# A graph layer on one core: edge groups in pairs, 24 of 32 rows stored, and the last chunk's node sums by a product on chip

## The chip, the cores and the metric

The kernel runs on one core of one Trainium2 chip. Its time is the device time of one execution in microseconds (us), the median of several runs. All arithmetic is in 32-bit floating point. TensorE is called PE here, VectorE DVE, ScalarE ACT, GpSimd POOL and SyncE SP.

## The reference

One layer over 10000 nodes of 512 features, with 160000 edges. The edges are sorted by `dst`; the graph sum of a node collects the transformed rows of its edges.

```python
xn = layernorm(x)                                   # 10000 x 512
h = xn @ gnn_W
agg = segment_sum(h[src] * edge_weight[:, None], dst)   # 160000 edges
gnn = relu(agg + gnn_bias)
mix = gamma_layernorm(linear_attention(xn, w_qkv, 8 heads) @ w_out.T, gamma)
x = x + gnn + mix
f = layernorm(x)
# one mixture of 6 experts for the whole input: router on the mean row, top 2
x = x + sum_e weight[e] * (gelu(f @ W1[e] + b1[e]) @ W2[e] + b2[e])
```

The kernel sums the rows of `xn` first and multiplies the sums by `gnn_W` afterwards. In the queries, the softmax is over the features of a head, in the keys over all nodes.

## The kernel before

**Nodes.** The 10000 rows are cut into 20 chunks: 19 of 512 rows (128 partitions by 4 rows, `SUB`), and a last one of 272 (68 by 4).

**Edges.** The edges lie in 1250 tiles of 128 edges. A *window* is a stretch of 32 (`WIN`) consecutive nodes; the first 384 windows (`PAIRED`) take two tiles each, the 482 later ones one tile each, 866 windows in all (`NW`). Four windows (`GROUP`) make a *group*, so there are 217 groups (`NQ`): 96 of eight tiles and 121 of four. `edges_in` issues, for each tile, one indirect DMA on POOL's queue (line 584) that gathers 128 rows of `xn` from memory (`msg`, 256 KB), and builds on DVE the 0/1 selection times the edge weight (`sel`, lines 590 and 592). `edges_summed` multiplies them on PE (line 602): four products with 32 output rows each, side by side in four column strips of the array. ACT copies the 128x512 result (`part`, line 605) and stores it to `part_d` (line 606), 256 KB a group. Where a node's edges go over the border of two windows, `carry` adds the first four rows of one window to the next, in memory, by an accumulating DMA on POOL's queue (line 674); `CARRIES` says at which windows such a carry is issued.

**Three stages.** In the first (to about 1110 us) keys and queries of all chunks are computed, the queries are turned and stored, and the context is summed. In the second, the row loop (about 1110 to 1905 us), each chunk gets its attention output (`attention`, product `po`), its node sums (`gathered`: an indirect DMA on POOL's queue, line 1018, that fetches rows of `part_d` by the list `row_of`; then a transpose, `at` to `aT`, and the product `pg` with `gnn_W`), bias, relu, the sum with `x`, and the row statistics for the next layer norm. `attention` runs three chunks ahead (`MIXED`). In the third stage, the feed-forward (from 1919 us), each chunk's rows come back from memory (`rows_in`), are normalised on ACT and turned on DVE (line 367), and go through the experts' products (line 243) in a form that needs fewer products and sums of weights made once (`sums_of_weights`, `w1_sum`).

**The order of the work.** PE's order is the order in which the program emits the instructions. The other engines are ordered by a planner that uses estimated costs; `behind(a, b)` ties one instruction behind another on its engine. The products of the edges are spread over the other products: after each product, `put_out` calls `work(us)`, which adds the product's estimated time and calls `edges_to` up to the group that is due at `ROW_PACE` = 0.96 us a tile. Before group i is multiplied, gathers are issued until more than `LATE` = 4 messages are held ready. `far_enough(c)` brings in the edges that chunk c's gather needs: `AT_HAND` lists up to which window the first n chunks need them. The last two chunks need all of them, so at chunk 17 (`NCH - 3`) `all_edges_in` multiplies all remaining groups in one go, issues the last carry, frees the edges' memory and loads the experts' weights; the gathers of chunks 18 and 19, and then the attention of chunk 19, follow.

In the trace, the visits to the edges in the row loop are of one group, except for a burst of four groups before the gather of chunk 17 and one of six at the end.

Of the kernel before, what the change touches and what calls it, by code (L numbers as in the profile page):

```python
# [17 lines left out]
P = 128  # L18
SQ = 32
# [6 lines left out]
GROUP = 4  # L26
WIN = P // GROUP
FAR = 1.0e5
EARLY = 2
# [6 lines left out]
ROW_PACE = 0.96  # L36
LATE = 4
MIXED = 3

AT_HAND = [(5, 320), (7, 384), (8, 424), (9, 472), (10, 520), (11, 560), (12, 604), (13, 640), (14, 680), (15, 716), (16, 752),  # L40
           (17, 788), (18, 820)]
CHAINED = 128
# [9 lines left out]
    (2, 2, 2), (2, 2, 1, 1), (2, 1, 1, 1, 1), (1, 1, 1, 1, 1, 1),  # L52
]


@with_exitstack
def gps_layer_kernel(
# [90 lines left out]
    NQ = -(-NW // GROUP)  # L148
    ZERO_ROW = NQ * P
    far_rows = -(-(N + P) // (8 * P)) * 8 * P  # L150
# [73 lines left out]
    def sums_of(o, a11, a12, a21, a22):  # L224

        nc.vector.tensor_tensor(o[0], a21, a22, ALU.add)  # L226
        nc.vector.tensor_tensor(o[2], a11, a21, ALU.subtract)  # L227
        nc.vector.tensor_tensor(o[1], o[0], a11, ALU.subtract)  # L228
        nc.vector.tensor_tensor(o[3], a12, o[1], ALU.subtract)

# [148 lines left out]
    def sums_of_weights():  # L379
        w1_sb, w1_sum = held_w["w1"], held_w["w1_sum"]  # L380
        p_half, q_half = slice(0, PAIRS * P), slice(PAIRS * P, 2 * PAIRS * P)
        sums_of([w1_sum[:, i] for i in range(4)], w1_sb[:, :KH, p_half], w1_sb[:, KH:, p_half],
                w1_sb[:, :KH, q_half], w1_sb[:, KH:, q_half])
# [4 lines left out]
    with ExitStack() as ph:  # L388
# [50 lines left out]
        jump = b_io.tile([P, NW], F32, name="jump")  # L439
        count = ep.tile([P, 3 + len(AT_HAND) + 2 * NCH], F32, name="count")  # L440
        small_norms = ep.tile([P, 2, KB], F32, name="small_norms")
        usable = ep.tile([P, 1], F32, name="usable")
        n_odd = ep.tile([1, 1], I32, name="n_odd")

        def edges_listed():
# [8 lines left out]
        def place_edges(dst_sb, row_sb):  # L454
# [16 lines left out]
            def by_window_of(t, per_window, o, op):  # L471
# [30 lines left out]
            yield  # L502
            nc.vector.scalar_tensor_tensor(good, place, float(WIN), good, op0=ALU.is_lt, op1=ALU.mult,
                                           accum_out=count[:, 0:1])
            yield
            nc.vector.tensor_scalar(good[:, :NW], gap, 0.0, None, op0=ALU.is_ge)
            yield
            nc.vector.scalar_tensor_tensor(good[:, : NW - 1], gap[:, : NW - 1], float(WIN // SUB), good[:, : NW - 1],
                                           op0=ALU.is_lt, op1=ALU.mult, accum_out=count[:, 1:2])
            yield  # L510
# [12 lines left out]

        def window_at(node, more):
            tile_no = NET * (node / N) ** 0.5 + more
            return min(max(int(tile_no / 2 if tile_no < 2 * PAIRED else tile_no - PAIRED), 0), NW)

        def span(c):
            return window_at(chunks[c][0], -SPARE), window_at(chunks[c][0] + SUB * chunks[c][1], SPARE)

        def spans_hold():
            for c, (b, r) in enumerate(chunks):
                for i, w, op, edge in ((0, span(c)[0], ALU.is_le, b), (1, span(c)[1], ALU.is_ge, b + SUB * r)):
                    at = 3 + len(AT_HAND) + 2 * c + i
                    nc.vector.tensor_scalar(count[:, at : at + 1], bases[:, w : w + 1], float(edge // SUB), None, op0=op)
# [60 lines left out]
        def edges_summed(i, batch, m, sel):  # L596

            pm = psum_e.tile([P, D], F32, name="pm")
            for j in range(batch):
                for h in range(GROUP):  # L600
                    k = h * batch + j
                    nc.tensor.matmul(pm[h * WIN : (h + 1) * WIN, :], sel[:, k, :], m[k] if k < len(m) else m[0],  # L602
                                     start=j == 0, stop=j == batch - 1, skip_group_check=True)
            part = pools["w"].tile([P, D], F32, name="part")
            nc.scalar.copy(part, pm)  # L605
            nc.scalar.dma_start(part_d[i * P : (i + 1) * P, :], part)

# [28 lines left out]
        def oddities():  # L636
# [8 lines left out]
            nc.vector.tensor_tensor(n_odd, n[:, 0:1], n[:, 1:2], ALU.add)  # L645

        def next_nodes():
            pn = psum.tile([P, 1], F32, name="pnext", tag="ps")
            nc.tensor.transpose(pn[:CHAINED], bases[0:1, 1 : CHAINED + 1], ident[0:1, 0:1])
            nc.vector.tensor_copy(nexts[:CHAINED], pn[:CHAINED])  # L650
# [25 lines left out]

        carried = []
        for i in range(PARTS):
            carried.append((past(CHAINED // GROUP, i * LAG), partial(carry_loads, i)))
            carried.append((past(CHAINED // GROUP, (i + 1) * LAG), partial(carry_chained, i)))  # L680
# [4 lines left out]
        pace = [PACE]  # L685
        ahead = [AHEAD]
        EARLY_TOTAL = PRODUCT * KB * ROWS_IN * 3 * KB

# [10 lines left out]
        def work(us):  # L699

            done[1] += us
            if not pools:

                normal_rows(int(done[1] / EARLY_TOTAL * (NCH + 1)) + 4 - len(normal))
                return
            edges_to(groups_of(int(done[1] / pace[0])))

# [13 lines left out]
        def all_edges(fp):  # L721
# [10 lines left out]
            for b in range(0, far_rows // P, 8):  # L732
                nc.sync.dma_start(view[:, b : b + 8, :], zero[:, None, :].to_broadcast([P, 8, D]))
            nc.vector.tensor_copy(row_of, four)
            dst_sb = fp.tile([P, NET], I32, name="dst_far")
            nc.sync.dma_start(dst_sb, dst)
# [120 lines left out]
        for c, (_, r) in enumerate(chunks):  # L857
# [51 lines left out]
            for cb in range(KB):  # L909
# [11 lines left out]
                if cb == KB // 2 - 1:  # L921
                    qT = b_io.tile([P, KB, SUB * P], F32, name="qT")
                    transposed(qT, qt, r, psum, "ps", by_act=range(KB) if c < EARLY else (1, 3))
                    nc.scalar.dma_start(qT_d[c], qT[:, :, : SUB * r])
            if c == CHECKED:
                next_nodes()
                oddities()
            if c >= CHECKED:
                find_rows(c, added)
                if c < 2 * CHECKED:  # L930
                    find_rows(c - CHECKED, added)
# [53 lines left out]
        pace[0] = ROW_PACE  # L985
        ahead[0] = LATE
        done[1] = tiles_of(done[0])[0] * ROW_PACE

# [8 lines left out]
        def far_enough(c):  # L997

            for n, w in AT_HAND:
                if c < n:  # L1000
                    edges_to(min(NQ, past(w // GROUP, lag_of(w) + LEAD) + 1))
                    return w * WIN
            assert not pools
            return ZERO_ROW + P

        def all_edges_in():
            edges_to(NQ)
            carry(CARRIES[-1], NW - 1)
            assert not carried
            pools.clear()  # L1010
            edge_ctx.close()
            experts_weights()

        def gathered(c):
            r = chunks[c][1]
            n_rows = far_enough(c)
            at = io.tile([P, SUB, D], F32, name="at", tag="at" if c < NCH - 1 else "qT")
            nc.gpsimd.indirect_dma_start(
# [20 lines left out]
        def attention(c, beside):  # L1039


            r = chunks[c][1]
            qT, xt = held.pop("last") if c == NCH - 1 else (queries_in(c), rows_again(c))
            ot = io.tile([P, SUB, D], F32, name="ot", bufs=MIXED + 2)
# [19 lines left out]
        for c, (_, r) in enumerate(chunks):  # L1064
            ot, at = mixed.pop(0), ats.pop(0)
            aT = io.tile([P, KB, SUB * P], F32, name="aT", bufs=1)

            if c == NCH - 3:
                all_edges_in()
                ats += [gathered(c + 1), gathered(c + 2)]  # L1070

            def nodes_rows():
                transposed(aT, at, r, psum, "ps", by_act=range(KB))

            if c + MIXED < NCH - 1:
                mixed.append(attention(c + MIXED, nodes_rows))
            elif c == NCH - 3:
                mixed.append(attention(NCH - 1, nodes_rows))
            else:
                nodes_rows()  # L1080
            if c < NCH - 3:
                ats.append(gathered(c + 1))
            if c == NCH - 4:
                held["last"] = queries_in(NCH - 1), rows_again(NCH - 1)

            for s in range(SUB):
                po = psum.tile([P, D], F32, name="pg", tag="ps")
                times(po, aT, s, r, wg)
                put_out(KB * PRODUCT)
                nc.vector.tensor_tensor(po[:r, :], po[:r, :], bias_b[:r], ALU.add)  # L1090
                nc.vector.scalar_tensor_tensor(ot[:r, s, :], po[:r, :], 0.0, ot[:r, s, :], op0=ALU.max, op1=ALU.add)
# [16 lines left out]
            if c == NCH - 3:  # L1108
                sums_of_weights()
            if c == NCH - 2:  # L1110
                io_f["in"] = ctx.enter_context(tc.tile_pool(name="f_in", bufs=1, reuse_waits="tile"))

                io_f["squares"] = io_f["in"].tile([P, P // SQ, P], F32, name="squares")
                for b in range(P // SQ):
                    nc.vector.tensor_copy(
                        io_f["squares"][:, b].rearrange("k (g t) -> k g t", t=SQ),
                        ident[:, None, b * SQ : (b + 1) * SQ].to_broadcast([P, P // SQ, SQ]))
                xn = rows_in(0)
                st = small.tile([P, P // SQ, 1, SUB, 2], F32, name="st_sq", bufs=1)
                stats_of_squares(st, 0)  # L1120
                for step in normalising(0, xn, st[:, :, 0]):
                    step()
                turn = turned_in(0, rows_turned(0, xn))
        in_order.close()
# [349 lines left out]
```

## Time and profile before

| | us |
|---|---|
| median of 3 runs | 3501.84 (3490.08 to 3503.91) |
| the profiled execution's own time | 3295.9 |
| its span, first to last instruction | 3294.2 |
| PE busy / POOL busy / DVE busy / ACT busy | 3187.5 / 1317.8 / 1772.1 / 834.1 |
| row loop's last edge product ends | 1845.0 |
| last product of the row loop ends | 1905.5 |
| first product of the feed-forward starts | 1919.0 |

The mean granted clock of TensorE in the profile is 0.985 of full speed. A view of groups gives for each kind of instruction its number, its busy time and mean duration in nanoseconds, and the idle time of its engine just before it with what ended that time. In a timeline, a line is a run of like instructions: its start, its length, and in brackets the idle time ahead of it. A matmul in 32-bit floating point shows as two records, and products with 32 output rows run four at a time.

### The profile page before, as it was taken

To read this page: it belongs to the slowest core of one execution; us is meant where nothing else is said; L and a number is where in the kernel's file an instruction comes from. 1 tells how busy PE (TensorE), PEld (TensorE's weight loads), DVE (VectorE), ACT (ScalarE), POOL (GpSimd) and SP (SyncE) were. 2 spreads that over 40 slices of the span, in tenths; PEclk is the share of its full clock that TensorE was granted. 3 is DMA by queue.
4 is the path that set the end of the run, shared out by engine and by line. 5 is a ranking of instruction groups with operands and counts; after the bars stand their busy time and mean duration, and the time that the engine had idled before them with its cause. 6 is when DMAs were issued, how large, how long until landed. Compare 5 with 4: busy or idle time off the path is not lost. (4 is left out here: it accounts for less than half of the span.)

```text
span 3294.2 us, 35223 instructions
## 1 busy us (share of the span) xinstructions
PE 3187.5 (97%) x12819; PEld 1898.0 (58%) x12819; DVE 1772.1 (54%) x3902; ACT 834.1 (25%) x1674; POOL 1317.8 (40%) x1421
## 2 busy tenths in 40 slices
PE   5899999999999999999999979999999999999998
PEld 3344444444443333333333358888888888888886
DVE  6655555555555366666665665455544554445532
ACT  5422222222222122222222132222222222222211
POOL 3377777777776777777777200000000000000000
PEclk8899999999999999999999989999999999999999
DMA  9678889888888999999999822121212212121111
GB/s 391 245 238 282 265 274 311 265 281 255 283 267 240 344 353 355 337 350 351 354 338 313 230 67 62 52 90 52 64 52 76 66 52 64 52 90 51 54 38 41
DMA packets 216728, 654.33 MB, mean 199 GB/s; under 512 B 34425, under 2 KB 74361, under 8 KB 188831
## 3 DMA queue, kind: packets, MB, share of 16 engines
q0 software_dynamic: 104096, 354.29, 32.9%
q1 hardware_dynamic: 69992, 175.33, 16.2%
q10 hardware_dynamic: 42452, 122.31, 9.6%
q8 instruction: 105, 1.72, 0.2%
q14 instruction: 83, 0.68, 0.1%
HBM read 491.21 MB, written 166.63 MB: 200 GB/s over the span
## 5 line engine op out<-in xcount | busy, mean ns | idle before, releaser
L584 POOL DMA_INDIRECT msg<-xn_d,src_sb x1250 | 1237.6, 990 | 422.9 <-issue 318.4
L602 PE MATMUL pm<-msg,sel 128*32 128x512 f32 x2504 | 357.7, 604 | 15.4 <-DMA msg<-xn_d,src_sb 14.4
L209 PE MATMUL pg<-wq,aT 128*128 128x512 f32 (+1 forms) x640 | 292.2, 604 | 0.0
L209 PE MATMUL po<-G,qT 128*128 128x512 f32 (+1 forms) x640 | 290.3, 600 | 1.4 <-DMA qT<-qT_d 1.4
L912 PE MATMUL pc<-xn,ek 128*128 128x512 f32 (+1 forms) x640 | 285.5, 596 | 0.0
L605 ACT COPY part<-pm 128x512 f32<-128x512 f32 x217 | 127.0, 585 | 618.3 <-PE pm L602 577.4
L602 PEld LDWEIGHTS pm<-msg,sel 128*32 128x32 f32 x2504 | 67.0, 109 | 273.0 <-issue 190.5
L209 PEld LDWEIGHTS pg<-wq,aT 128*128 128x128 f32 (+1 forms) x640 | 115.5, 188 | 176.1 <-issue 161.2
L243 PE MATMUL px<-xnT,w_sb 128*128 128x256 f32 (+1 forms) x800 | 204.9, 379 | 7.0 <-DVE u L1291 6.6
L209 PEld LDWEIGHTS po<-G,qT 128*128 128x128 f32 (+1 forms) x640 | 114.8, 187 | 164.7 <-issue 157.8
L166 DVE BATCH_NORM_STATS2 st<-ot 128x6 f32<-128x512 f32 (+1 forms) x160 | 110.4, 690 | 180.1 <-ACT ot L1053 179.3
L243 PE MATMUL p<-kq_sum,xs_b 128*128 128x512 f32 (+1 forms) x432 | 200.7, 600 | 0.0
L912 PEld LDWEIGHTS pc<-xn,ek 128*128 128x128 f32 (+1 forms) x640 | 118.0, 191 | 139.3 <-issue 131.4
L243 PE MATMUL px<-w_sb,hh 128*128 128x256 f32 (+1 forms) x800 | 185.8, 379 | 0.0
L243 PE MATMUL py<-xs,w_sum 128*128 128x256 f32 (+1 forms) x800 | 185.7, 375 | 0.0
L243 PE MATMUL py<-w_sum,hh 128*128 128x256 f32 (+1 forms) x800 | 179.2, 379 | 0.0
L243 PEld LDWEIGHTS px<-xnT,w_sb 128*128 128x128 f32 x800 | 150.8, 192 | 30.1 <-DVE u L1291 10.2
L243 PEld LDWEIGHTS px<-w_sb,hh 128*128 128x128 f32 (+1 forms) x800 | 150.2, 188 | 22.8
L243 PEld LDWEIGHTS py<-w_sum,hh 128*128 128x128 f32 (+1 forms) x800 | 150.0, 188 | 22.7
L243 PEld LDWEIGHTS py<-xs,w_sum 128*128 128x128 f32 x800 | 150.2, 191 | 20.1
L243 PEld LDWEIGHTS p<-kq_sum,xs_b 128*128 128x128 f32 (+1 forms) x432 | 78.0, 187 | 116.1 <-issue 89.6
L351 ACT ACTIVATE xn<-xn,st_all 128x128 f32<-128x128 f32 x288 | 114.8, 481 | 97.3 <-DMA xn<-x_d 97.3
(298 smaller groups left out, 4566.8 us busy)
## 6 DMA issues: line engine op xcount, KB each, us to landing
part_d<-part ACTq DMA_DIRECT2D x217, 256.0 KB
msg<-xn_d,src_sb POOLq DMA_INDIRECT x1250
xn<-in_x SPq DMA_DIRECT2D x19, 1024.0 KB
xn_d<-xn ACTq DMA_DIRECT2D x19, 1024.0 KB
qT_d<-qT ACTq DMA_DIRECT2D x19, 1024.0 KB
qT<-qT_d SPq DMA_DIRECT2D x19, 1024.0 KB
xt<-in_x SPq DMA_DIRECT2D x19, 1024.0 KB
x_d<-ot SPq DMA_DIRECT2D x19, 1024.0 KB
```

The costliest lines, as they stand in the source:

```text
L166: nc.vector.bn_stats(st[:r, s, :], t[:r, s, :])
L209: nc.tensor.matmul(po[:r, :], t[:, kb, s * r : (s + 1) * r], w[:, kb, :], start=kb == 0, stop=kb == KB - 1)
L243: nc.tensor.matmul(o, lhs[j], rhs[j], start=start and j == 0, stop=stop and j == n - 1, skip_group_check=True)
L351: nc.scalar.activation(xn[:, s, b * P : (b + 1) * P], xn[:, s, b * P : (b + 1) * P], AF.Identity, bias=st[:, b, s, 0:1], scale=st[:, b, s, ...
L584: nc.gpsimd.indirect_dma_start(out=m[k], out_offset=None, in_=xn_d, in_offset=bass.IndirectOffsetOnAxis(ap=src_sb[:, t0 + k : t0 + k + 1], ...
L602: nc.tensor.matmul(pm[h * WIN : (h + 1) * WIN, :], sel[:, k, :], m[k] if k < len(m) else m[0], start=j == 0, stop=j == batch - 1, skip_gro ...
L605: nc.scalar.copy(part, pm)
L912: nc.tensor.matmul(pc, ek[:r, s, cb * P : (cb + 1) * P], xn[:r, s, :], start=s == 0, stop=s == SUB - 1)
```

## The change

- **Groups in pairs.** In the row loop `work` advances the edges in steps of `VISIT` = 2 groups, and `LATE` is 8 for 4.
- **24 rows of 32.** From window 384 on (one tile per window), only 24 rows (`USED`) of a window are stored, by four DMAs per group on ACT's queue, where there was one. The check at the start that a tile's nodes fit its window is made with 24 for these windows. The eight rows that are not stored are set to zero once, after chunk 5 (`rest_cleared`: a memset on POOL and 16 DMAs on ACT's queue).
- **The last chunk on chip.** Groups from 211 on (`ON_CHIP`) keep their sums in the buffers `parts`; groups 214 to 216 are not stored at all. `nodes_on_chip` works out, once, which node each of their rows belongs to, `numbered` makes of it a 0/1 matrix per group, and `last_sums` multiplies the kept sums with it: this gives chunk 19's turned node sums directly. Two calls: for the first four groups (`FIRST_SUMS`), at the end of chunk 17; for the other two in chunk 19, where rows gathered from memory are added too (in the ordinary case all of them zero).
- **The end of the edges.** `AT_HAND` gets the entry (19, 853), so chunk 18 does not wait for all edges. At chunk 17 the edges run on with its products up to group 214, then come the first sums, and `all_edges_in` with the last two groups. The attention of chunk 19 moves ahead to chunk 16.
- **The way into the feed-forward.** The rows of chunk 0 are loaded in `all_edges_in`, ahead of the weights. `sums_of_weights` moves from chunk 17's end to chunk 18's, and the bias additions of chunk 19 are tied behind it on DVE.

```diff
-LATE = 4
+LATE = 8
+VISIT = 2
+FIRST_SUMS = 4
-           (17, 788), (18, 820)]
+           (17, 788), (18, 820), (19, 853)]
+    ON_CHIP = window_at(N, NET, chunks[-1][0], -3) // GROUP
+    STORED = -(-CARRIES[-1] // GROUP)
...
             nc.scalar.copy(part, pm)
-            nc.scalar.dma_start(part_d[i * P : (i + 1) * P, :], part)
+            if batch > 1:
+                nc.scalar.dma_start(part_d[i * P : (i + 1) * P, :], part)
+            elif i < STORED:
+                for h in range(GROUP):
+                    nc.scalar.dma_start(by_window[i * GROUP + h, :USED, :], part[h * WIN : h * WIN + USED, :])
...
+        def rest_cleared():
+            zero = pools["w"].tile([P, PER, D], F32, name="none", tag="on", bufs=1)
+            nc.gpsimd.memset(zero, 0.0)
+            for w in range(PAIRED, STORED * GROUP, P):
+                end = min(w + P, STORED * GROUP)
+                for q in range(USED, WIN, PER):
+                    nc.scalar.dma_start(by_window[w:end, q : q + PER, :], zero[: end - w])
...
-            edges_to(groups_of(int(done[1] / pace[0])))
+            stop = min(groups_of(int(done[1] / pace[0])), limit[0])
+            edges_to(done[0] + (stop - done[0]) // visit[0] * visit[0])
...
             if c == CHECKED:
+                rest_cleared()
+                nodes_on_chip()
...
         def all_edges_in():
             edges_to(NQ)
-            carry(CARRIES[-1], NW - 1)
+            ats.append(gathered(NCH - 2))
+            ats.append(gathered(NCH - 1))
...
+            io_f["in"] = ctx.enter_context(tc.tile_pool(name="f_in", bufs=1, reuse_waits="tile"))
+            rows_first = rows_in(0)
             experts_weights()
...
+        def numbered():
+            b, r = chunks[-1]
+            mine = io.tile([P, NQ - ON_CHIP + 1, SUB, r], F32, name="mine", tag="xt", bufs=1)
+            number = mine[:, NQ - ON_CHIP]
+            nc.gpsimd.iota(number, pattern=[[1, SUB], [SUB, r]], base=b, channel_multiplier=0,
+                           allow_small_or_imprecise_dtypes=True)
+            for g in range(NQ - ON_CHIP):
+                nc.vector.tensor_scalar(mine[:, g], number, node_of[:, g : g + 1], None, op0=ALU.is_equal)
+            return mine
+
+        def last_sums(o, mine, groups, at):
+            n = SUB * chunks[-1][1]
+            for kb in range(KB):
+                kbs = slice(kb * P, (kb + 1) * P)
+                pt = psum.tile([P, SUB * P], F32, name="pt", tag="ps")[:, :n]
+                for g in groups:
+                    nc.tensor.matmul(pt, parts[g // 3][:, g % 3, kbs], mine[:, g].rearrange("p s n -> p (s n)"),
+                                     start=g == groups[0], stop=at is None and g == groups[-1], skip_group_check=True)
+                if at is None:
+                    nc.scalar.copy(o[:, kb, :n], pt)
+                    continue
+                r = chunks[-1][1]
+                for s in range(SUB):
+                    nc.tensor.matmul(pt[:, s * r : (s + 1) * r], at[:r, s, kbs], ident[:r, :r],
+                                     start=False, stop=s == SUB - 1, skip_group_check=True)
+                nc.vector.tensor_tensor(o[:, kb, :n], o[:, kb, :n], pt, ALU.add)
...
-            if c + MIXED < NCH - 1:
+            if c + MIXED < NCH:
                 mixed.append(attention(c + MIXED, nodes_rows))
-            elif c == NCH - 3:
-                mixed.append(attention(NCH - 1, nodes_rows))
+            elif c < NCH - 1:
+                nodes_rows()
             else:
-                nodes_rows()
+                last_sums(aT_last, mine, range(FIRST_SUMS, NQ - ON_CHIP), at)
...
+            if c == NCH - 3:
+                limit[0] = ON_CHIP + FIRST_SUMS
...
+                if c == NCH - 1:
+                    behind(added, weights_summed)
...
             if c == NCH - 3:
-                sums_of_weights()
+                mine = numbered()
+                aT_last = io.tile([P, KB, SUB * P], F32, name="aT_last", tag="ot", bufs=MIXED + 2)
+                edges_to(limit[0])
+                last_sums(aT_last, mine, range(FIRST_SUMS), None)
+                rows_first = all_edges_in()
             if c == NCH - 2:
...
-                turn = turned_in(0, rows_turned(0, xn))
+                turn = turned_in(0, rows_turned(0, rows_first))
+                weights_summed = sums_of_weights()
```

## The prediction

> **What bounds the kernel now.** I start with the busy tenths of 40 slices (82.4 us each).
>
> ```profile
> PE   5899999999999999999999979999999999999998
> POOL 3377777777776777777777200000000000000000
> DMA  9678889888888999999999822121212212121111
> ```
>
> PE is full nearly everywhere, but POOL stands at 7 from about 165 us to 1840 us, and 7 is all it can show: the timeline of POOL has a message gather of 0.95 us and then 0.30 us of issue before the next. So I asked for POOL's groups in 1095 to 1840 us, the row loop that the change touches.
>
> ```profile
> L584 POOL DMA_INDIRECT msg<-xn_d,src_sb x530 | 529.4, 999 | 174.6 <-issue 134.7 <-DMA msg<-xn_d,src_sb 19.6 <-PE po L209 5.9
> L1018 POOL DMA_INDIRECT at<-part_d,row_of x18 | 17.0, 945 | 12.1 <-DMA part_d<-part_d 4.7 <-issue 4.3 <-DMA msg<-xn_d,src_sb 1.9
> L674 POOL DMA_DIRECT2D part_d<-part_d x12 | 11.7, 974 | 0.0
> ```
>
> In each: instructions, busy us, mean ns of one, idle us just before and what ended it. And three stages, as start:end, length, then busy us of PE, PEld, DVE, ACT and POOL, PE's clock, DMA share and GB/s:
>
> ```profile
> 1400.00:1500.00 100.00, 100.00 (x359) 38.89 (x360) 61.56 (x161) 24.56 (x47) 74.95 (x76) 1.00 0.97 352
> 1820.00:1840.00 20.00, 15.05 (x47) 3.70 (x45) 10.08 (x26) 2.55 (x5) 14.49 (x15) 0.91 0.97 323
> 1900.00:1920.00 20.00, 6.48 (x15) 2.38 (x14) 15.04 (x30) 6.41 (x17) 0.00 (x0) 0.74 0.47 148
> ```
>
> Busy plus idle of POOL's three groups is 529.4+174.6+17.0+12.1+11.7 = 744.8 us of 745: POOL never rests. Its 530 messages take 1.33 us each, where the bare spacing is 1.25 us. DMA is at 0.97. PE is "100" busy too, but its edge products (L602) take 22.5 us per 100 us there (the mean of seven such stretches), against 18 visits of 1.07 = 19.3: the 3.2 between are waits inside the bars, 23 us over the loop. **POOL's issue of messages sets the end of the edges; PE and DMA are close behind.** Next, PE's timeline: what a visit to the edges costs, and the way out of the loop.
>
> ```profile
> 1408.15 3.70 PE L209 MATMUL po<-G,qT 128*128 128x512 f32 x8
> 1411.78 1.06 PE L602 MATMUL pm<-msg,sel 128*32 128x512 f32 x8
> 1412.78 3.70 PE L209 MATMUL po<-G,qT 128*128 128x512 f32 x8
> ...
> 1011.07 1.88 PE L243 MATMUL p<-kq_sum,xnT 128*128 128x512 f32 x4
> 1012.88 1.92 PE L602 MATMUL pm<-msg,sel 128*32 128x512 f32 x16
> 1014.73 1.22 PE L201 MATMUL pt<-ident,xn 68*128 68x68 f32 x16
> ...
> 1825.27 4.18 PE L602 MATMUL pm<-msg,sel 128*32 128x512 f32 x24
> ...
> 1839.45 5.63 PE L602 MATMUL pm<-msg,sel 128*32 128x512 f32 x16 [0.35 <-DMA msg<-xn_d,src_sb]
> 1845.01 10.52 PE L209 MATMUL po<-G,qT 128*68 128x512 f32 x24
> ...
> 1919.02 2.05 PE L243 MATMUL px<-xs,w_sum 128*128 128x256 f32 x4 [13.52 <-DVE xs L235]
> ```
>
> And POOL's timeline, its last message:
>
> ```profile
> 1837.81 0.95 POOL L584 DMA_INDIRECT msg<-xn_d,src_sb  x1 [0.30 <-issue]
> ```
>
> The last message is issued at 1837.8+0.95 = 1838.8, PE's last edge product ends at 1845.0, and then come 59 us of products that need no message (chunk 19's attention, the products of chunks 17 to 19, up to 1905.5) and a hole of 13.5 us until the feed-forward stage begins at 1919.0. The burst of six groups from 1825.3 to 1845.0 took 19.7 us for 6x0.857+0.35 = 5.5 us of products, one of four before it 12.6 for 3.8: 23 us of waiting for messages.
>
> [...] from one L209 start to the next across a visit is 1412.78-1408.15 = 4.63 us; eight records of 0.4285 us are 3.43, so one group costs 1.20; two groups' worth at 1012.88 cost (1014.73-1011.07)-4x0.4285 = 1.95, not 2.40. [...]
>
> **The change part by part**, against the profiled execution (3295.9 us, span 3294.2). The median of the timed runs, 3501.84, is 6.2% above it; no view says where, so I carry the result over as a ratio.
>
> *Two groups at once.* By following the emission in the code, the row loop makes 116 visits of one group and three larger ones now, 64 of two afterwards: 58x(2x1.20-1.95) = 26 us less PE time. While POOL bounds, PE only waits longer for messages, so I count 0 and keep 26 for the range. The wider look-ahead (8 for 4) puts more messages ahead of each gather of rows on POOL; POOL's pauses of over 0.6 us beyond the bare spacing add up to about 18 us in this window; I take 8 off, bounds 0 and 15.
>
> *24 rows of 32.* Each stored group becomes four DMAs on ACT's queue: 118 groups, 3x118 = 354 more issues of 0.33 us (median of L606) = 117 us of ACT's sequencer over 740 us, where ACT is 25% busy. Bytes: 118x64 KB = 7.7 MB less in the loop; [...] I count 0 (bounds: 0 to 7.7 MB/350 GB/s = 22 us off). The same 7.7 MB return as clears: 16 DMAs of 512 KB on ACT's queue after chunk 5 (near 361 us), POOL at its limit and DMA at 0.84. [...] in the waits of SP's queue loads of x wait for unrelated loads:
>
> ```profile
> SPq L416 <- DMA wk<-in_w_qkv_t: 2.8, 1, 2.8
> SPq L416 <- DMA wq<-in_w_qkv_t: 2.4, 1, 2.4
> SPq L416 <- DMA gamma_b<-in_gamma: 1.7, 1, 1.7
> ```
>
> so I estimate that ACT stands until the first half has landed: 4 MB at 150 GB/s = 27 us (352/0.97 = 363 GB/s is DMA's full speed; 273 at 0.83 are used then; the spare 90 and half of 363 bracket the 150). Exponentials and evictions queue behind it, and PE runs dry after about eight products and a visit, 9 us: PE loses 18 us, which its slack in the row loop (23 inside the bars, 23 in bursts, 26 from visits) swallows. What stays is POOL: messages slowed for 30 to 50 us. I take 7 us, bounds 0 and 20. The zero memset on POOL and the iota later: 2 us.
>
> *Last chunk on chip, edges in the loop.* Attention of chunk 19 (16 products, 13.7 us, with 4 ACT evictions) and chunk 17's transposes and products (15.5 us) move ahead of the last message, as do the first node sums: 16 of 24 products of 272 columns, 2x0.228 us each = 7.3 us. PE's 72 us of slack stand against these 36.5 and the 18 above, so POOL stays the bound. On the way out: last message issued 1838.8-8+7+2 = 1839.8. Groups 213 and 214 end six messages earlier plus 5.5 us to land (1838.8 to 1844.3 now): 1838. Then two products of chunk 17 (6.9) and the first sums (7.3): 1852; the last two groups: 1854. Chunk 18's rows: the carry waits for group 213's stores (6 us now, 1846 to 1852), then 5 us to the gather's issue (1852.1 to 1857.2), some 10 to land: 1860, so PE waits 6 us, a new wait with all of the remaining PE order behind it. Transposes and products 15.6, statistics 0.8, second sums and addition 6, products of chunk 19 13.9: 1897; one more for the switch: **1898** against 1919.0. The hole of 13.5 us goes because chunk 0's rows are loaded before the weights: four SP DMAs (4.9 us for two now, L328) are put ahead of sixteen weight loads. These start at 1854+5 and took 26 us (1845.1 to 1871.2): 1885, and w1's sums 4x1.48 = 6: 1891. The pinned order makes the last chunk's bias additions wait for these sums: covered by 7 us while chunk 19's products run; without that cover, PE stands at PSUM. At nothing: the split checks and the 18 small node-number operations (DVE 55% busy around 380 to 480 us), the 6 comparisons, one find_rows fewer. Chunk 19's statistics now share DVE with the first feed-forward chunk: +2.
>
> Sum: -21+2 = **-19 us, -0.58%: 3482 us** (the -8, +7 and +2 are within the 21). Alone, this case reaches from 3465 to 3498.
>
> **Rivals.** *PE or DMA decides.* If TensorE runs slower in the timed runs, messages are early and visits count: -26, sums +12, the hole -13.5, burst waits -12: about -40, 3460. For it: PE at 9 in every slice; against: the waits in L602. Full relief by the bytes gives the same size. *Hidden.* If the additions to the last chunk's sums stand behind w1's sums on DVE, chunk 19's products start at 1892 or later: -6, 3495. *Slower: ACT's queue.* [...] eight stores a visit meet three 1 MB transfers on SP per chunk. At d us of PE time for each of 51 meetings it costs 51d; from d = 0.4 the gain is gone; d = 0.8 is +41: +22 in all, 3525. For it: four issues per group in front of the evictions; against: today one store in 128 of the loop was late by over 3 us.
>
> **How the numbers follow.** A measurement here can tell about 0.5%. POOL-bound 0.45 (split 0.30 faster, 0.13 within, 0.02 slower), PE or DMA 0.25 (faster), hidden 0.10 (0.01, 0.08, 0.01), ACT 0.20 (0.04 within, 0.16 slower). Sums: faster 0.56, same 0.25, slower 0.19. Range 3440 (both relief terms) to 3532 (ACT at d = 1).
>
> **What would show it.** L602 in visits of 16 records spaced by 1.95 us; POOL full to about 1840 us with the last message within 8 us of 1838.8; PE's feed-forward start (L243 px) near 1898 with no 13.5 us wait on xs, but one of some 6 us on the rows of chunk 18; near 365 us a PE wait of 10 to 25 us behind ACT. A last message before 1825 or after 1850, or L209 products waiting on ACT in the loop, would prove the account wrong.

## The result, and the profile after

| | kernel before | changed kernel | ratio (95% interval) |
|---|---|---|---|
| first runs, ten each | 3493.4 us | 3524.32 us | 1.0091 (1.0064 to 1.0118) |
| set with its parts, 25 and 5 runs | 3297.04 us | 3311.82 us | 1.0047 (1.0033 to 1.0061) |
| once more, 12 and 5 runs | 3295.58 us | 3310.82 us | 1.0044 (1.0031 to 1.0058) |

The change makes the kernel slower: by 31 us in the first ten runs, where both kernels take 6% more time, and by 15 us in the later sets. The experiments below, and the profile that the prediction was read from, go with the later sets. The profile of the changed kernel that came with the first ten runs (span 3533.3 us) shows waits of PE that no other profile here does; the columns are total us, times, and the longest:

```profile
PE pt L211 <- issue: 34.1, 39, 4.0
PE pm L614 <- issue: 23.3, 31, 2.2
PE pg L219 <- issue: 23.2, 13, 7.7
```

"issue" is time in which PE waited for nothing that the profile shows, and the profile of before has no such rows. So that page can't be laid beside the one of before; from here the same kernel is shown as it ran with its parts (span 3309.7 us, against 3298.1 for the kernel before in the first experiment). Its lines are numbered ten or more higher; L596 is the message gather, L614 the edges' product, L219 `po` and `pg`, L253 the products that were L243.

The busy tenths, each slice 82.7 us:

```profile
PE   6889999999999999999999899999999999999998
POOL 3367777777776777777777300000000000000000
DMA  9688888888888999999999642121212212121111
```

PE and POOL lost a tenth in the third slice (165 to 248 us), and PE one more in slice 23 (1820 to 1903 us), which was full; slice 24, with the old hole, is full now. In between neither moved. POOL's groups in the row loop, 1105 to 1850 us, confirm that: the same 530 messages, as tightly packed as before, only ten microseconds later.

```profile
L596 POOL DMA_INDIRECT msg<-xn_d,src_sb x530 | 528.6, 997 | 180.0 <-issue 132.4 <-DMA msg<-xn_d,src_sb 27.9 <-DMA at<-part_d,row_of 5.6
L1109 POOL DMA_INDIRECT at<-part_d,row_of x18 | 17.0, 943 | 8.6 <-issue 5.4 <-DMA part_d<-part_d 1.1 <-DMA msg<-xn_d,src_sb 0.6
L721 POOL DMA_DIRECT2D part_d<-part_d x12 | 11.7, 978 | 0.0
```

PE's timeline: a visit of two groups, and the way out of the loop.

```profile
1394.88 3.60 PE L219 MATMUL pg<-wq,aT 128*128 128x512 f32 x8
1398.41 1.92 PE L614 MATMUL pm<-msg,sel 128*32 128x512 f32 x16
1400.26 7.13 PE L219 MATMUL pg<-wq,aT 128*128 128x512 f32 x16
...
1853.24 1.11 PE L211 MATMUL pt<-ident,at 128*128 128x128 f32 x4 [6.35 <-DVE ot L1180]
1860.30 8.84 PE L219 MATMUL pg<-wq,aT 128*128 128x512 f32 x16 [5.94 <-ACT aT L213]
...
1888.33 1.94 PE L211 MATMUL pt<-ident,at 128*128 128x128 f32 x16 [1.09 <-DMA at<-part_d,row_of]
...
1925.67 1.03 PE L253 MATMUL px<-xs,w_sum 128*128 128x256 f32 x4
```

The visit costs 1400.26-1394.88-8x0.4285 = 1.95 us, as foretold. The feed-forward begins without the hole of 13.5 us that stood there, but at 1925.7, not at 1898. Two waits of 12.3 us together, inside chunk 17's rows, are new. Three other engines show where they come from; this is POOL's end of the messages, then DVE, then ACT:

```profile
1850.84 0.95 POOL L596 DMA_INDIRECT msg<-xn_d,src_sb  x1 [0.30 <-issue]
1851.80 0.39 POOL L1082 IOTA mine<- 128x272 f32 x1
```

```profile
1852.22 0.36 DVE L1085 TENSOR_SCALAR mine<-mine,node_of 128x272 f32<-128x272 f32 x1 [13.16 <-POOL mine L1082]
```

```profile
1859.57 0.20 ACT L184 ACTIVATE root<-ve 128x4 f32<-128x4 f32 x1 [15.54 <-DVE ve L179]
```

The iota of the node numbers takes 0.39 us, but it lies on POOL's queue behind the last message. It waited for the queue alone, as far as the trace shows: the iota's tile takes over the buffer of `xt`, but DVE, which reads `xt`, had ended its last instruction at 1852.22-13.16 = 1839.1, 12.7 us before the iota began. DVE stands 13.2 us in front of the first comparison that needs the iota, and the relus of chunk 17 are queued behind that comparison. Their inputs stay in PSUM, and PE stands 6.35 us for DVE's `ot`. ACT's square root for the row statistics then waits 15.5 us for DVE, with the copies of `aT` queued behind it: the second wait of PE, 5.94 us.

The other loss is near 180 us: the clears. Lines of POOL, of ACT and its queue, and of PE, and last POOL's line at this place in the kernel before:

```profile
183.28 0.98 POOL L688 MEMSET none<- 128x1024 f32 x1
197.68 0.95 POOL L596 DMA_INDIRECT msg<-xn_d,src_sb  x1 [13.42 <-PE pm L614]
```

```profile
184.28 1.59 ACTq L692 DMA_DIRECT2D part_d<-none  x3
186.25 0.69 ACT L949 ACTIVATE ek<-p,usable 128x512 f32<-128x512 f32 x1 [21.67 <-issue]
```

```profile
186.99 3.78 PE L253 MATMUL p<-kq_sum,xs_b 128*128 128x512 f32 x4 [9.30 <-ACT ek L949]
```

```profile
185.44 0.94 POOL L584 DMA_INDIRECT msg<-xn_d,src_sb  x1 [2.21 <-PE pm L602]
```

The planner moved the clears from their place in the program (after chunk 5, near 361 us) to the start of the edges. ACT's queue reached them at 164.0 and stood until 184.3: the memset of the zeros, 0.98 us of work, lay on POOL behind the first 24 messages. An exponential was queued behind the clears, PE ran dry and stood 9.3 us for it, no message buffer came free, and POOL itself then paused for 13.4 us, where it had paused for 2.2.

### The profile page after: what moved, and what is told of

Same layout as the page of the kernel before. It is cut to its first block, busy times and chain, and to the rows that moved or that the text cites. A ratio compares the mean times of both kernels' runs of the same rounds, so it can differ in the third digit from the quotient of the medians.

```text
span 3533.3 us, 35772 instructions
## 1 busy us (share of the span) xinstructions
PE 3273.8 (93%) x12883; PEld 1944.0 (55%) x12883; DVE 1770.6 (50%) x3930; ACT 826.4 (23%) x1674; POOL 1315.4 (37%) x1423
## 5 line engine op out<-in xcount | busy, mean ns | idle before, releaser
L596 POOL DMA_INDIRECT msg<-xn_d,src_sb x1250 | 1234.3, 987 | 649.9 <-issue 336.6
L614 PE MATMUL pm<-msg,sel 128*32 128x512 f32 x2504 | 349.6, 611 | 29.9 <-issue 23.3
L964 PE MATMUL pc<-xn,ek 128*128 128x512 f32 (+1 forms) x640 | 308.8, 631 | 19.6 <-issue 12.2
L219 PE MATMUL pg<-wq,aT 128*128 128x512 f32 x608 | 287.5, 623 | 30.8 <-issue 23.2
L219 PE MATMUL po<-G,qT 128*128 128x512 f32 (+1 forms) x640 | 296.1, 609 | 16.7 <-issue 13.7
L614 PEld LDWEIGHTS pm<-msg,sel 128*32 128x32 f32 x2504 | 74.0, 110 | 279.9 <-issue 257.2
L219 PEld LDWEIGHTS pg<-wq,aT 128*128 128x128 f32 x608 | 115.8, 197 | 201.5 <-issue 180.3
L219 PEld LDWEIGHTS po<-G,qT 128*128 128x128 f32 (+1 forms) x640 | 119.4, 192 | 180.7 <-issue 172.8
L253 PE MATMUL px<-xnT,w_sb 128*128 128x256 f32 (+1 forms) x800 | 205.4, 380 | 12.5 <-DVE u L1377 12.5
L253 PE MATMUL p<-kq_sum,xs_b 128*128 128x512 f32 (+1 forms) x432 | 204.3, 606 | 13.2 <-ACT ek L949 10.6
L253 PE MATMUL px<-w_sb,hh 128*128 128x256 f32 (+1 forms) x800 | 185.7, 379 | 0.0
L253 PE MATMUL py<-xs,w_sum 128*128 128x256 f32 (+1 forms) x800 | 185.4, 375 | 0.0
L253 PE MATMUL py<-w_sum,hh 128*128 128x256 f32 (+1 forms) x800 | 179.2, 379 | 0.0
L253 PEld LDWEIGHTS px<-xnT,w_sb 128*128 128x128 f32 x800 | 150.5, 192 | 36.7 <-DVE u L1377 17.2
L602 DVE TENSOR_TENSOR sel<-iota_w,place 128x128 f32<-128x128 f32 (+2 forms) x217 | 73.4, 341 | 189.3 <-remote 54.4
L253 PE MATMUL p<-wk,xnT 128*128 128x512 f32 (+1 forms) x288 | 144.1, 624 | 23.0 <-issue 13.8
L253 PEld LDWEIGHTS py<-w_sum,hh 128*128 128x128 f32 (+1 forms) x800 | 150.1, 188 | 22.6
L253 PEld LDWEIGHTS px<-w_sb,hh 128*128 128x128 f32 (+1 forms) x800 | 150.1, 188 | 22.6
L253 PEld LDWEIGHTS py<-xs,w_sum 128*128 128x128 f32 x800 | 149.9, 191 | 19.9
```

The lines of the kernel that those rows point to most:

```text
L219: nc.tensor.matmul(po[:r, :], t[:, kb, s * r : (s + 1) * r], w[:, kb, :], start=kb == 0, stop=kb == KB - 1)
L253: nc.tensor.matmul(o, lhs[j], rhs[j], start=start and j == 0, stop=stop and j == n - 1, skip_group_check=True)
L596: nc.gpsimd.indirect_dma_start(out=m[k], out_offset=None, in_=xn_d, in_offset=bass.IndirectOffsetOnAxis(ap=src_sb[:, t0 + k : t0 + k + 1], ...
L602: nc.vector.tensor_tensor(sel[:, :n], iota_w[:, None, :].to_broadcast([P, n, WIN]), place[:, t0 : t0 + n, None].to_broadcast([P, n, WIN]), ...
L964: nc.tensor.matmul(pc, ek[:r, s, cb * P : (cb + 1) * P], xn[:r, s, :], start=s == 0, stop=s == SUB - 1)
```

## The experiments

Each ratio is to the kernel before in runs beside it. "The new end" means the last three points of the change: the last chunk on chip, the end of the edges, and the way into the feed-forward.

**The kernel before itself**, to place the 6%.

> The kernel before, unchanged, to get a profile of it in the condition of the timed runs. The profile of before that the prediction used (3295.9 us) is 6% under all ten timed runs of it (3457 to 3506). Theory A (the 6% is a general slowing of instruction issue, no matter which kernel): this run takes 3460 to 3510 us and its first stage, which the change hardly touches, shows PE waits on issue and ends as late as in the changed kernel (about 1290 us for the last context product, against 1090 in the old profile). Theory B (the change itself slows the first stage): this run's first stage ends 30 us or more before that of the changed kernel.

Measured: 3299.9 us, and the 27 runs beside it have a median of 3296.51. The kernel before takes what its own profile said, so the 6% belongs to the time or place of the first runs, not to the kernel. Neither theory of what slows them could be tried, since no later run took that long.

**Parts taken back.** Three kernels in one set.

```diff
# without pairs
-LATE = 8
-VISIT = 2
+LATE = 4
+VISIT = 1
# full rows, no clears
-                for h in range(GROUP):
-                    nc.scalar.dma_start(by_window[i * GROUP + h, :USED, :], part[...])
+                nc.scalar.dma_start(part_d[i * P : (i + 1) * P, :], part)
...
-                rest_cleared()
# the new end alone: both edits
```

> The changed kernel with groups one at a time and the old look-ahead (VISIT 1, LATE 4). If the pairs are the loss (8 messages must be there at once, two results and eight stores meet on ACT), this is 15 to 35 us faster than the changed kernel. If, as forecast, the pairs save PE time and PE bounds in these runs, it is 15 to 30 us slower. If the loss lies in the stores and clears, it moves by under 10 us.

> The changed kernel with all 32 rows stored by one DMA per group and without the clears; pairs and the new end stay. Theory stores (clears hold ACT from 163 to 204 us in the changed kernel's trace, and four stores per group delay ACT's evictions): 30 to 60 us faster than the changed kernel, so 0 to 30 us under before. Rival (bytes in the row loop matter, DMA being nearly full there): slower than the changed kernel by 10 to 20 us.

> The kernel before with the new end alone: last chunk's sums on chip, edges ending with the loop's products, chunk 0's rows loaded ahead of the weights; groups one at a time, 32 rows stored. The forecast's account of the end gives 20 to 30 us under before. If the new end has put a new wait in the place of the old one, it is within 10 us of before.

Measured: without pairs 3313.33, 1.0049 (1.0036 to 1.0062); full rows 3297.97, 0.9999 (0.999 to 1.0007); the new end alone 3296.85, 1.000 (0.9991 to 1.001). So the stores or the clears cost about 14 us (not the 30 to 60 expected after the first ten runs), pairs move nothing, and the new end, which was to bring 21 us, brings nothing either. Its trace has no clears, and still shows the wait at the iota, on DVE first and then on PE:

```profile
1844.12 0.36 DVE L1083 TENSOR_SCALAR mine<-mine,node_of 128x272 f32<-128x272 f32 x1 [16.28 <-POOL mine L1080]
```

```profile
1845.14 1.11 PE L211 MATMUL pt<-ident,at 128*128 128x128 f32 x4 [5.13 <-DVE ot L1178]
...
1850.44 5.75 PE L219 MATMUL pg<-wq,aT 128*128 128x512 f32 x8 [1.51 <-DVE ot L1178]
```

**The changed kernel beside its repairs.** The first is unchanged; the second moves one memset; the third adds clears to the new end, where nothing needs them; the fourth takes the iota out of the way in the new end.

```diff
# memset on DVE
-            nc.gpsimd.memset(zero, 0.0)
+            nc.vector.memset(zero, 0.0)
# clears added to the new end
             if c == CHECKED:
+                rest_cleared()
# number early, into a tile of its own
-            number = mine[:, NQ - ON_CHIP]
-            nc.gpsimd.iota(number, ...)
...
+        number = small.tile([P, SUB, chunks[-1][1]], F32, name="number", bufs=1)
+        nc.gpsimd.iota(number, ...)
         mixed = [attention(c, lambda: None) for c in range(MIXED)]
```

> The changed kernel itself, in one set with its parts. Sum of the parts so far: stores and clears with the new end 1.0049 of before, pairs on top of full rows and the new end nothing. Additive: 1.004 to 1.006. Rival, pairs and four stores per group hurt one another (eight stores in a visit ahead of ACT's next eviction): 1.008 to 1.010, as in the first ten runs.

> The changed kernel with one word changed: the zero memset of the clears on DVE instead of POOL. Theory clears: ACT's queue stands for 20 us because the memset lies behind the messages on POOL, and this costs PE and POOL some 10 us for good; then 8 to 12 us less than the changed kernel, about 1.002 of before. Rival, the sixteen clears themselves hold ACT's queue, whatever they wait for: 0 to 4 us less. Rival, the four stores per group are the cost: no difference.

> The new end with full rows stored by one DMA a group and single visits, plus the clears, which are not needed there. Theory clears: 10 to 14 us more than the new end alone (which was 1.000 of before), so 1.003 to 1.004. Theory stores (four DMAs a group cost the 16 us): within 2 us of the new end alone, 1.000.

> The new end alone, but the iota of the node numbers is issued into a tile of its own before the row loop, so it no longer lies behind the last messages on POOL with DVE waiting for it (16.3 us in the new end alone, of which PE stood 8.2). Theory iota: 8 us less, 3289, 0.9975 of before. Rival, DVE's chain after the last edges (weights' sums, then chunk 19's statistics) sets the feed-forward's start anyway: 0 to 2 us less, 0.9995 to 1.000.

Measured:

| | us | ratio |
|---|---|---|
| changed kernel | 3311.82 | 1.0047 (1.0033 to 1.0061) |
| memset on DVE | 3300.68 | 1.0010 (1.0004 to 1.0017) |
| new end and clears | 3313.94 | 1.0042 (1.0028 to 1.0056) |
| new end, number early | 3282.18 | 0.9956 (0.9943 to 0.9970) |

The clears alone carry the loss that the first set left between stores and clears, and one memset moved from POOL to DVE gives 11.1 us of it back. With it there the zeros are ready at 164.4 us, and ACT's next exponential waits 4.6 us instead of 21.7:

```profile
168.77 0.69 ACT L949 ACTIVATE ek<-p,usable 128x512 f32<-128x512 f32 x1 [4.57 <-DMA part_d<-none]
```

The same sixteen transfers are still issued between 164.4 and 192 us, and PE no longer waits for ACT there. POOL's pause is 1.1 us, and the last message starts at 1839.9 us instead of 1850.8. The early iota gives the new end 0.44%, 14.5 us, more than the 8.2 us for which PE stood in that trace. Most of the rest is that the products behind the stands took longer: from chunk 17's last transposes to the next group of edges PE took 17.2 us with the late iota (1838.97 to 1856.12) and takes 5.3 us here (1832.60 to 1837.88), and the same eight records of `pg` that took 5.75 us take 3.60. What is left is no more than single traces differ by: the last message starts at 1842.7 with the late iota, at 1837.8 here, and at 1839.9 and 1847.8 in two kernels below that differ from this one only behind it. The way out of the loop with the early iota:

```profile
1789.35 1.83 PE L614 MATMUL pm<-msg,sel 128*32 128x512 f32 x2 [2.66 <-DMA msg<-xn_d,src_sb]
...
1834.35 3.60 PE L219 MATMUL pg<-wq,aT 128*128 128x512 f32 x8
...
1897.95 1.03 PE L253 MATMUL px<-xs,w_sum 128*128 128x256 f32 x4
...
1908.18 2.07 PE L253 MATMUL px<-xnT,w_sb 128*128 128x256 f32 x4 [4.88 <-DVE u L1375]
```

**Both repairs, and the stores.** Four kernels in one set: the whole change with the memset on DVE and the early iota; full rows with pairs and early iota; the same with each stored group in four DMAs of 32 rows; and the new end with early iota where chunk 0's rows are loaded behind the weights.

```diff
# four of 32
-                nc.scalar.dma_start(part_d[i * P : (i + 1) * P, :], part)
+                for h in range(GROUP):
+                    nc.scalar.dma_start(by_window[i * GROUP + h, :, :], part[h * WIN : (h + 1) * WIN, :])
# rows late
-            rows_first = rows_in(0)
             experts_weights()
+            rows_first = rows_in(0)
```

> The changed kernel whole, with two edits: the zero memset on DVE, and the iota of the node numbers before the row loop. If the two waits on POOL are all that was wrong with it: 1.001 (memset on DVE alone) less the 14.7 us that the early iota gave the new end alone, 3286, 0.9966 of before. Rival, the stores of 24 rows by four DMAs hold back chunk 18's rows or the evictions as soon as the iota is out of the way: 0.999 to 1.001.

> Full rows by one DMA a group, no clears, double visits, the early iota. Pairs worth nothing while POOL bounds: the same as single visits with the early iota, 0.9956 (3282). Rival, pairs give PE room in the row loop that was hidden behind the wait at the iota: 5 to 15 us less, 0.991 to 0.994.

> As the kernel with full rows, pairs and early iota, but each stored group of four tiles goes out by four DMAs of 32 rows: the changed kernel's number of issues without its saving of bytes and without clears. Theory, neither issues nor bytes count ([...]ACT has room): within 3 us of one DMA a group. Rival, two terms cancelled in the changed kernel, fewer bytes against more issues: 8 to 22 us slower than one DMA a group.

> The new end alone with the early iota, but chunk 0's rows are loaded behind the experts' weights again. Theory, the hole ahead of the feed-forward was closed by loading the rows first: DVE's sums of the turned rows are done 7 us before PE needs them now and would come about 25 us later (the weights' loads), less what of it statistics wait for anyway: PE waits 8 to 15 us ahead of its first feed-forward product, ratio 0.998 to 1.000. Rival, the hole was closed by the last chunk's own shorter path and the rows land early either way: 0.9955 as without the edit.

Measured:

| | us | ratio |
|---|---|---|
| whole change, both repairs | 3285.0 | 0.9961 (0.9949 to 0.9974) |
| full rows, pairs, number early | 3282.4 | 0.9956 (0.9944 to 0.9968) |
| the same, four DMAs of 32 rows | 3287.76 | 0.9972 (0.9962 to 0.9982) |
| new end, number early, rows late | 3295.09 | 0.9995 (0.9986 to 1.0003) |

With both waits gone the whole change is faster than the kernel before. Pairs are again worth nothing (0.9956 with and without). Four issues a group seem to cost about 5 us against one, between the 3 of the theory and the 8 of the rival, but the intervals overlap at their ends. Whether 24 rows with their clears are better than four stores of 32 (by 3 us here), these runs don't resolve. The stores' own rows, in the order one store of 128 rows, whole change, four of 32 (number, then min/median/max in ns of one issue on ACT's queue):

```profile
L626 ACTq DMA_DIRECT2D part_d<-part x115: 325/326/1526, 1174.7 to 1813.3; - x115
```

```profile
L627 ACTq DMA_DIRECT2D part_d<-part x460: 295/378/2162, 1178.9 to 1824.6; - x154
```

```profile
L627 ACTq DMA_DIRECT2D part_d<-part x460: 308/434/2024, 1176.1 to 1822.4; - x154
```

With the rows late the hole is back: 13 us in the time (3295.09 against 3282.18), 16.0 in the trace:

```profile
1924.23 2.05 PE L253 MATMUL px<-xs,w_sum 128*128 128x256 f32 x4 [16.03 <-DVE xs L245]
```

**The tie, and the changed kernel again.**

```diff
-                if c == NCH - 1:
-                    behind(added, weights_summed)
```

> The new end alone with the early iota, without the tie of chunk 19's bias additions behind w1's sums on DVE. In the trace with the tie, the feed-forward begins at 1897.95 and then waits 4.9 us for DVE, which has the additions and statistics of chunk 19 in hand; its second pair starts 14.9 us after the first, against 10.4 before. Theory, the tie makes these 5 us: gone, 3277 (0.994). Rival, DVE has the same work to do in either order, and the sums come as much later as the additions come earlier: PE waits ahead of its first feed-forward product instead, within 2 us of 0.9956.

> The changed kernel once more, to see whether its distance to the kernel before depends on where both run: 1.0091 in the ten first runs, when both took 6% more time, 1.0047 in the set with its parts. Theory, the two waits on POOL cost a fixed amount and the rest comes from that slower condition: 1.004 to 1.0055 again if the kernel before takes about 3297 us. Rival, the first ratio is the right one and the second fell low by chance: 1.007 to 1.010.

Measured: untied 3287.11, 0.9974 (0.9963 to 0.9984); the changed kernel 3310.82, 1.0044 (1.0031 to 1.0058). Without the tie PE stands in front of its first feed-forward product:

```profile
1909.38 2.05 PE L253 MATMUL px<-xs,w_sum 128*128 128x256 f32 x4 [9.13 <-DVE w_sum L238]
```

Both numbers missed. The tie doesn't cost 5 us; it seems to save about 5, though the intervals overlap at their ends. The rival's mechanism is what the trace shows: DVE is late at the seam in either order, and without the tie PE stands 9.1 us ahead of its first product instead of 4.9 a little later. The second ratio of the changed kernel repeats, so about 1.0045 is its ratio in these sets.

## Why the prediction was wrong, step by step

The forecast was 0.58% faster and the result is slower. Added up from medians of the later sets:

| part | us | from |
|---|---|---|
| new end, free of the iota's wait | -15 | 0.9956 |
| pairs | 0 | 0.9956 with and without |
| stores of 24 rows, clears without the wait | +3 | 3285.0-3282.4 |
| DVE and PE behind the iota on POOL | +16 | 1.0010-0.9961 |
| ACT behind the memset on POOL | +11 | 3311.82-3300.68 |
| sum | +15 | measured 14.8 |

From the second row on, each row compares two kernels that differ in that one part, so the sum has to come out; by the intervals, a row is good to some 4 to 6 us.

- **The step that failed** is the sentence "The zero memset on POOL and the iota later: 2 us". It priced the two instructions by their time on POOL (0.98 and 0.39 us) and put the waits of other engines for them at nothing. These waits are what they cost: 11 and 16 us. The view needed was in the prediction already: POOL never rests. The memset came out at 183.3 us, behind 24 messages, and ACT's queue had stood for it since 164.0; the iota came out at 1851.8, behind the last message, and DVE had stood 13.2 us for it.
- **Clears.** The total was within its bounds, the mechanism was not. I had ACT stand 27 us for half of the clears' transfers to land, which was an estimate; it stood 20.3 us for the memset (164.0 to 184.3), and about 4.6 us for the transfers once the memset was out of the way. I let PE's 18 us be swallowed by its slack in the row loop and kept 7 for POOL, from slower messages. But PE's stand of 9.3 us left the message buffers full, and POOL, the bound itself, paused for 13.4 us waiting for PE's edge product: that pause stays, and the last message is issued at 1850.8+0.95 = 1851.8 against 1839.8. A last message after 1850 was the prediction's own sign of being wrong. The place was wrong too (184 us, not 361): the planner is free to hoist what depends on nothing.
- **The new end** met its forecast in part by luck. With the early iota, the last message is issued by 1838.9 and the feed-forward begins at 1897.95, where 1898 was foretold. The hole went because the rows come first (loaded late, they bring back a wait of 16.0 us). But POOL was to set the pace to its last message, and it doesn't: PE stands for a message for the last time at 1789.35, and from there its own products fill the time but for 0.6 us. So the last two groups end at 1859.8 instead of 1854, while chunk 18's rows cost PE not 6 us but nothing (1.1 in the changed kernel); the two errors offset one another.
- **DVE at the seam**, put at +2, was +4.6: the second pair of the feed-forward starts 14.9 us after the first, where it was 10.4. Without the tie it is 10.7, but PE then stands 9.1 us ahead of the first: the tie only moves the place.
- **Pairs and LATE.** The saving per visit was right (1.95 us for two), its worth of 0 as well. The 8 us for the wider look-ahead are not there: 0 for both edits together.
- **24 rows.** The count of 0 for bytes was my estimate. It stands within 3 us (3285.0 against 3287.76 with four stores of 32 rows); why, no run shows. The issues, taken as free, seem to cost about 5 us. If that is the rival of ACT's queue, it is small: 5.4 us over 51 meetings is 0.1 us each, below its 0.4. ACT's copies of `part` stood 136 us in all behind stores in the changed kernel, 88.5 with four stores of 32 rows and 7 with one store of 128; beside the 5 us of the last two kernels, nearly all of that standing costs nothing.
- **The two other rivals** found no support: neither less PE time for the visits nor fewer bytes showed in the time, and the additions to the last sums were not held behind the weights' sums.
- **Left open**: the further 0.45% of the first ten runs, some 16 us. Both waits are in their profile too, in much the same size: POOL pauses 13.7 us after the memset, and on the way out of the loop PE stands 10.4 us, as these lines show.

```profile
2078.97 0.66 PE L211 MATMUL pt<-ident,at 128*128 128x128 f32 x4 [4.03 <-issue]
2086.03 8.96 PE L219 MATMUL pg<-wq,aT 128*128 128x512 f32 x16 [6.40 <-ACT aT L213]
```

So the two waits are there as well, but they don't explain the rest. The feed-forward of that profile lasts 1381 us (2151.9 to 3533.3) and the other 1384, so its extra time lies in the two stages with the edges, where the rows "issue" stand. There is no trace of the kernel before from those runs, so which step loses more in them isn't known. To carry the ratio from the one profile to the other runs was thus unsound, by as much as the loss itself.

## What to carry to other kernels

Price an instruction on a saturated queue by who waits for its result, not by its length: a memset of 1 us and an iota of 0.4 us cost this kernel 27 us. Constants that depend on nothing belong before the queue fills, or on an engine with room (the memset was done at 164.4 us on DVE, at 184.3 on POOL); look also for where a planner may hoist the consumer. A stall of a following engine is not swallowed by its slack when full buffers carry it back to the engine that bounds, as PE's 9.3 us came back as POOL's 13.4.

## What the runs showed of the hardware

An issue on ACT's queue wasn't of one price here: 326 ns (median) for a store of 128 rows, 434 for one of 32 rows and 378 for one of 24, as the stores' rows show, so by these medians a store cut in four took the queue over four times as much.

Edge products, with 32 output rows, overlapped: in the kernel before, four of their records start together at 1411.8 us and last 617 ns each, and eight fill 1.06 us, where eight records of 128 output rows fill 3.70.

Some stands of PE cost more than their length here. In the changed kernel as it ran with its parts, the first four records behind the stand of 9.30 us for the exponential took 3.78 us and the next four 2.30, where four took 1.88 before it: 2.3 us more. Behind the 5.94 us for `aT`, sixteen records took 8.84 us, and 7.13 at 1870.92: 1.7 us more. The mean granted clock from 165.5 to 248.2 us was 0.94 in that trace and 1.00 in the kernel before. Two other profiles give the granted clock right behind a stand. In that of the first ten runs it was 0.50 from 187 to 191 us, behind 10.55 us for the same exponential, and 0.50 from 2086 to 2089 us, behind the 6.40 us for `aT`. In that of the kernel before it was 0.50 from 1919 to 1923 us, behind the hole of 13.52 us, and 1.00 from 1924 to 1930. The last four transposes of the way out took 1.11 us behind 6.35 us in the changed kernel as it ran with its parts, and 0.66 behind 4.03 us in the profile of the first ten runs.
